# Fourth mW1 unit expanded in place inside the first pair's second layer, and three more block products of that pair's first layer at two levels

## The chip, the cores and the metric

The kernel runs on one core of one Trainium2 chip. Its engines are TensorE (PE: matmuls; PEld: the loading of its weights), VectorE (DVE), ScalarE (ACT), GpSimd (POOL) and SyncE (SP, which only issues DMAs). Each executes its own queue in order and waits on semaphores for the others. The metric is the device time of one execution in microseconds (us); lower is better. All data are fp32.

## The reference, cut to what matters

The input x is four sequences of 512 tokens by 512 values. A conditional block is followed by an adapter per sequence:

```python
q, k, v = x @ Wq, x @ Wk, x @ Wv
attn = softmax(q k^T * V**-0.5)
attn_out = (attn @ v) @ Wp + bp
cms = gelu(attn_out @ cW1 + cb1) @ cW2 + cb2      # 512 -> 2048 -> 512
cms = cms + one_hot(target_codes)
modifier = gelu(concat(attn_out, cms) @ mW1 + mb1) @ mW2 + mb2   # 1024 -> 2048 -> 512
x = clip(x + cms + modifier, 0, 1)
# adapter, its weights picked by stream[b]
h = x + gelu(x @ Wd + bd) @ Wu + bu
out = layernorm(h) * g + b
```

## The kernel before

**Products.** Nearly every large matrix product is done in the Strassen-Winograd way: the operands are cut into 2 by 2 blocks, and seven block products replace eight. Each block product needs sums of weight blocks (made by `weight_sums`, L239 to L244) and sums of token blocks (`token_sums`, L249). The seven products have the numbers 1 to 7. Three of them (1, 2, 4) take a plain weight block; 3, 5, 6 and 7 take a sum. "Two levels" means that a block product is itself cut into seven smaller ones, which takes inner sums of both operands. Sums of the weights for several layers are made once by POOL (the "expansion", `expand`, L378 to L410), in units of 256 weight columns or rows, written to DRAM (`c1_inner`, `c1_outer`, `c2_kept`, `m1_kept`, `m2_kept`) and loaded again by SP when they are used. Four weight tiles, `wslot0` to `wslot3`, are used in turn (`next_weights`).

**Order of the work.** First comes the attention of all four sequences, in two pairs. Then, for each pair of sequences, four layers: c1 (`c1_layer`, cW1), c2 (`second_layer`, cW2), m1 (`m1_layer`, mW1) and m2 (`second_layer`, mW2). The adapters of the first pair run inside the second pair's c1, those of the second pair at the end. Within c1 the products come in the order `FIRST_C = (2, 1, 5, 6, 7, 3, 4)`, in c2 and m2 in the order (3, 1, 5, 6, 7, 2, 4), in m1 in the order (1, 5, 6, 7, 2, 3, 4).

**c1.** For the first pair, products 1 and 5 have two levels (`c1_two_level`, matmuls at L1229, 28 of 256 columns); 2, 6, 7, 3 and 4 have one (matmuls at L1319, 16 of 512 columns). For the second pair (`more`) all seven have two levels. There, the inner weight sums of 1, 2 and 5 are loaded from DRAM, those of 6, 7, 3 and 4 are made by POOL when they are needed (L1221), and the inner token sums are made by POOL too (L1168 to L1171); for the first pair the token sums are made by DVE (L249). `seven` (L592, L657) combines the partial products in PSUM with DVE and ACT; `combine_first_tile` (L1334) does it for the one-level products.

**Expansion.** `expansion()` has POOL expand cW1, two units of cW2 and four units of mW1. It runs beside the attention and the first pair's c1: after each step of c1 two steps of it are put into the program (`steps(between, 2)`). `late_expansion()` expands mW2 during the first pair's m1, and after it the inner sums of cW1's product 2 for the second pair (`expand_c1_late`, `C1_KEPT`). In the profiled execution, POOL works on the fourth mW1 unit from 296.5 to 336 us, and on nothing from then to 408 us.

**Second layers.** `second_operands` forms four difference blocks of the hidden values in place (L1407) and, for each product, the inner token sums (L249 into slots 4 to 7). In the first pair's c2 (`busy`) DVE makes all of these; in the other second layers the first difference is a negated copy by ACT to which a DMA adds the other block (L1447), and in the second pair's c2 POOL makes the first inner sums. The partial products are combined by DVE (`inner`, L1091), which empties the PSUM banks: seven per product, eight in all. The temporary of `inner` is the tile `mod[0]` in c2 and `first` in m2 and m1.

**Adapters.** `load_adapter` (gathers at L1559) issues 14 indirect DMAs on POOL's queue for each sequence, into slots 4 and 5 for one and 6 and 7 for the other, at the end of the first pair's m2. Those slots are m2's token sums until then.

**Queues.** A scheduler orders the instructions of each engine, except where `keep_in_program_order` or `issue_after` pins them. DMAs are issued on SP's queue (weights, attention results), ACT's and POOL's (expansion, adapters). An engine's queue isn't left for a later instruction while the one ahead of it waits.

Of the kernel before, what the change touches and what calls it, by code (L numbers as in the profile page):

```python
# [18 lines left out]
def kernel(  # L19
# [226 lines left out]
    def token_sums(b11, b12, b21, b22, t1, t2, t3, t4, eng=None, pinned=False):  # L246
# [12 lines left out]
    C1_BESIDE = (6, 7, 3, 4)  # L259
    C1_KEPT = (2,)  # L260
# [4 lines left out]
        for p, n in ((1, 1024), (5, 2048), (2, 1024))  # L265
# [35 lines left out]

    def expand_c1_late(raws, sums):

        units = [(p, u) for p in C1_KEPT for u in range(2)]

        def block_of(i):
            return raws[i % 4].rearrange("p (m c n) -> p m c n", m=2, c=2)

        def load(i):
            p, u = units[i]  # L310
            raw = block_of(i)
            if p in C1_SUM:
                nc.gpsimd.dma_start(out=raw, in_=c1_outer[u][:, C1_SUM[p]])
            else:
                for m in range(2):
                    nc.gpsimd.dma_start(out=raw[:, m], in_=c1_plain(p, u, m))

        def begin():
            for i in range(min(4, len(units))):
                load(i)  # L320

        def rest():
            for i, (p, u) in enumerate(units):
                raw = block_of(i)
                to = sums[i % 4].rearrange("p (k n) -> p k n", k=4)
                weight_sums(
                    raw[:, 0, 0], raw[:, 0, 1], raw[:, 1, 0], raw[:, 1, 1],
                    *(to[:, k] for k in range(4)),
                )
                if i + 4 < len(units):  # L330
                    load(i + 4)
                nc.gpsimd.dma_start(out=c1_inner[p, u], in_=sums[i % 4])
                yield

        return begin, rest()

# [112 lines left out]
    def expansion():  # L451

        c2_units = [(cW2, False, c2_kept, u) for u in range(2)]
        yield from expand_c1(0, lambda: load_c1(1, nc.gpsimd))
        yield from expand_c1(1, lambda: load_raw(cW2, False, 0, slot[4:6]))

        constants()
        yield from expand_all(
            c2_units + m1_units, slot[4:6], (flat(part), slot[3], slot[1]), flat(first)
        )  # L460

    def late_expansion():

        spaces = (flat(mod[0]), flat(mod[1]), slot[0])
        quarters = lambda tiles: [t[:, at : at + 1024] for t in tiles for at in (0, 1024)]
        begin, rest = expand_c1_late(quarters(slot[6:8]), quarters(spaces[:2]))
        yield from expand_all(m2_units, slot[6:8], spaces, None, begin)
        yield from rest
# [510 lines left out]
    for pair in range(B // 2):  # L979
# [78 lines left out]

        pair_product(lhs_vp, operands, attn, bp_c, then=then, at=pT[0] if pair else None)
# [7 lines left out]

    turns = [0]

    def next_weights():  # L1070
        turns[0] += 1
        return wslot[turns[0] % len(wslot)]
# [37 lines left out]
    def inner_operands(t, half, sums, eng=None, pinned=False):  # L1110

        b11, b12 = t[:, :half, :256], t[:, :half, 256:]
        b21, b22 = t[:, half:, :256], t[:, half:, 256:]
        t1, t2, t3, t4 = sums
        token_sums(b11, b12, b21, b22, t1, t2, t3, t4, eng, pinned)
        return {1: b11, 2: b21, 3: b22, 4: t4, 5: t1, 6: t2, 7: t3}

# [28 lines left out]
    in_rows = [t.rearrange("p (c n) -> p c n", c=4) for t in slot]  # L1146

    def load_attn(pair, slots=(0, 1)):
        for k, i in enumerate(slots):
            nc.sync.dma_start(out=in_rows[i], in_=attn_kept[2 * pair + k])  # L1150

    def c1_operands(slots=(0, 1, 2, 3)):


        at0, at1, t12, t34 = (in_rows[i] for i in slots)
        b11, b12, b21, b22 = at0[:, 0:2, :], at1[:, 0:2, :], at0[:, 2:4, :], at1[:, 2:4, :]
        t1, t2, t3, t4 = t12[:, 0:2, :], t12[:, 2:4, :], t34[:, 0:2, :], t34[:, 2:4, :]
        operands = {1: b11, 2: b21, 3: b22, 4: t4, 5: t1, 6: t2, 7: t3}

        def inner_sums(p, k, eng=None):  # L1160

            s = mod[1][:, 2 * k : 2 * k + 2, :].rearrange("p a (b n) -> p (a b) n", b=2)
            t = operands[p]
            s1, s2, s3, s4 = (s[:, i : i + 1, :] for i in range(4))
            if eng is None:
                return inner_operands(t, 1, [s1, s2, s3, s4], pinned=True)
            c11, c12, c21, c22 = t[:, :1, :256], t[:, :1, 256:], t[:, 1:, :256], t[:, 1:, 256:]
            eng.tensor_tensor(s1, c12, c11, ALU.subtract)  # L1168
            eng.tensor_tensor(s2, c22, s1, ALU.subtract)
            eng.tensor_tensor(s3, c22, c12, ALU.subtract)  # L1170
            eng.tensor_tensor(s4, c21, s2, ALU.subtract)  # L1171
            return {1: c11, 2: c21, 3: c22, 4: s4, 5: s1, 6: s2, 7: s3}

        def minus(out_, one, two):
            tc.keep_in_program_order(nc.vector.tensor_tensor(out_, one, two, ALU.subtract))

        minus(t1, b12, b11)

        def rest():
            minus(t2, b22, t1)  # L1180
            yield
            minus(t3, b22, b12)
            minus(t4, b21, t2)
            yield

        return operands, inner_sums, rest()

    def fetch(out, in_):

        tc.keep_in_program_order(nc.sync.dma_start(out=out, in_=in_))  # L1190

    def c1_two_level(p, h, rhs, after, beside):


        a = []
        for g in range(2):
            w = next_weights()
            if p == 5:
                fetch(out=w, in_=c1_inner[5, g])
            else:  # L1200
                if p in C1_SUM:
                    fetch(
                        out=w[:, :1024],
                        in_=c1_outer[g][:, C1_SUM[p]].rearrange("p m c n -> p (m c n)"),
                    )
                else:
                    for m in range(2):
                        fetch(
                            out=w[:, 512 * m : 512 * m + 512].rearrange("p (c n) -> p c n", c=2),
                            in_=c1_plain(p, g, m),  # L1210
                        )
                if p not in C1_BESIDE:
                    fetch(out=w[:, 1024:], in_=c1_inner[p, g])
            a.append(w.rearrange("p (k n) -> p k n", k=8))
        if p in C1_BESIDE:
            for out_, one, two, op in (
                (4, 2, 3, ALU.add), (5, 4, 0, ALU.subtract), (6, 0, 2, ALU.subtract),
                (7, 1, 5, ALU.subtract),
            ):
                for w in a:  # L1220
                    nc.gpsimd.tensor_tensor(w[:, out_], w[:, one], w[:, two], op)  # L1221
# [55 lines left out]
    def c1_layer(h, rhs, after, more, beside):  # L1277
# [11 lines left out]
        for p in FIRST_C:  # L1289
# [8 lines left out]
            for g in range(2):  # L1298
# [31 lines left out]
                if more:  # L1330
                    beside()
# [552 lines left out]
```

## Time and profile before

| | |
|---|---|
| median of 10 runs | 1163.84 us (1162.45 to 1164.31) |
| the profiled execution's own time | 1164.57 us |
| its span, first to last instruction | 1162.8 us |
| granted clock of TensorE, mean | 0.998 |
| first pair: c1 | 236.9 to 329.8 us |
| first pair: c2 | 329.8 to 416.4 us |
| first pair: m1, then m2 | 416.4 to 585.8, to 670.3 us |
| second pair: c1, with the first pair's adapters | 670.3 to 786.0 us |
| second pair: c2 | 786.0 to 870.6 us |
| longest wait of PE | 1.8 us, in the first pair's c2 |

The page of a profile has, in this order: the busy time of each engine, the span in 40 slices, the DMA queues, the chain of work that ended last, the costliest groups of instructions and the DMA issues. A group or a row of a timeline names the line of the kernel, the engine, the operation, the tile written and the tiles read, the shape and the count. An idle time in brackets names what ended it. A matmul of the program appears as two instructions (fp32). The name of a tile without its number stands for all tiles of the name: `wslot` for the four weight tiles, `wide` for slots 0 and 1.

### The profile page before, as it was taken

Reading aid. Unit: us, or ns where it says so; the run is one execution under the profiler, and the core shown is the slowest. Engines: PE = TensorE matmul, PEld = TensorE weight load, DVE = VectorE, ACT = ScalarE, POOL = GpSimd, SP = SyncE. Lnnn points to the kernel's source line nnn. Section 1 sums busy time; section 2 is a strip of 40 time slices with the busy share of each in tenths; the row PEclk is TensorE's granted clock in tenths of the full one; section 3 lists DMA queues with packets and bytes.
Section 4 is the critical chain, followed back from the end, with each engine's and each line's share of the span. In section 5 each row is a group of like instructions: output and inputs, shape, how many; then the busy total and the mean of one; then the engine's idle time right before and its main releaser. Section 6 shows DMA issues by size and latency. Waiting matters only on the chain.

```text
span 1162.8 us, 13672 instructions
## 1 busy us (share of the span) xinstructions
PE 1153.0 (99%) x4941; PEld 922.4 (79%) x4941; DVE 884.9 (76%) x1227; ACT 293.7 (25%) x535; POOL 587.6 (51%) x646
## 2 busy tenths in 40 slices
PE   9999999999999999999999999999999999999997
PEld 8588468566468888888888877778888888888875
DVE  6755755477699965898699956789994588689955
ACT  4234426235520000013310036372000003230014
POOL 4999979898950058864200767971000001165401
PEclk9999999999999999999999999999999999999999
DMA  9795494898775578897837562145645364675701
GB/s 281 266 251 198 183 395 153 337 371 284 270 268 235 170 264 315 302 336 304 262 130 305 177 205 91 65 163 196 265 160 184 145 237 161 185 268 199 252 2 72
DMA packets 101442, 258.88 MB, mean 223 GB/s; under 512 B 24532, under 2 KB 59648, under 8 KB 86144
## 3 DMA queue, kind: packets, MB, share of 16 engines
q1 hardware_dynamic: 77088, 157.17, 38.6%
q0 software_dynamic: 20848, 89.18, 21.6%
q10 hardware_dynamic: 3440, 11.67, 2.5%
q8 instruction: 39, 0.64, 0.2%
q14 instruction: 27, 0.22, 0.1%
HBM read 188.78 MB, written 66.06 MB: 219 GB/s over the span
## 4 chain that ended last, share of the span: by engine, by line
PE 95%; DVE 3%; DMA 1%; issue 1%; DVEq 0%
PE i L1387 28%; PE i L1487 28%; PE sum L748 10%; PE sum L1229 9%; PE sum L682 8%; PE c L1319 5%; PE down_ps L1594 2%; PE up_ps L1613 2%; DMA wslot<-in_L_cond_mW 1%; PE tr_ps L519 1%; DVE slot L249 1%; DVE wide L1407 1%; PE up_ps L1608 1%; DVE hidden L592 0%; PE tr_ps L935 0%
## 5 line engine op out<-in xcount | busy, mean ns | idle before, releaser
L1387 PE MATMUL i<-slot,wslot 128*128 128x256 f32 x1184 | 261.2, 379 | 0.1
L1387 PEld LDWEIGHTS i<-slot,wslot 128*128 128x128 f32 x1184 | 224.8, 190 | 31.2 <-DMA wslot<-in_L_cond_mW 0.5
L1487 PE MATMUL i<-slot,wslot 128*128 128x256 f32 x896 | 202.8, 379 | 1.8 <-DVE cms L1091 1.8
L1487 PEld LDWEIGHTS i<-slot,wslot 128*128 128x128 f32 x896 | 170.2, 190 | 25.3 <-DVE cms L1091 2.2
L1487 PE MATMUL i<-hidden,wslot 128*128 128x256 f32 x576 | 132.2, 379 | 0.0
L1487 PEld LDWEIGHTS i<-hidden,wslot 128*128 128x128 f32 x576 | 109.4, 190 | 15.7 <-issue 1.0
L1098 ACT COPY first<-i 128x512 f32<-128x512 f32 (+1 forms) x42 | 21.6, 515 | 390.3 <-PE i L1387 234.0
L1091 DVE TENSOR_TENSOR part<-i,part 128x512 f32<-128x512 f32 (+1 forms) x156 | 90.5, 591 | 36.9 <-PE i L1387 27.3
L1120 ACT ACTIVATE hidden<-hidden,bias 128x512 f32<-128x512 f32 x128 | 83.9, 716 | 73.7 <-DVE hidden L592 63.6
L1770 POOL DMA_DIRECT2D slot<-xT_kept x4 | 2.9, 727 | 152.9 <-PE i L1387 152.9
L1229 PE MATMUL sum<-mod,wslot 128*128 128x256 f32 x288 | 66.6, 379 | 0.0
L249 DVE TENSOR_TENSOR slot<-hidden 128x1024 f32<-128x1024 f32 x46 | 61.4, 1334 | 0.0
L1229 PEld LDWEIGHTS sum<-mod,wslot 128*128 128x128 f32 x288 | 54.7, 190 | 7.4
L1773 POOL TENSOR_TENSOR cms<-cms,slot 128x512 f32<-128x512 f32 x16 | 23.9, 1518 | 68.1 <-PE i L1387 38.5
L249 DVE TENSOR_TENSOR slot<-hidden,slot 128x1024 f32<-128x1024 f32 x46 | 56.7, 1232 | 0.3
L1091 DVE TENSOR_TENSOR part<-i,first 128x512 f32<-128x512 f32 (+1 forms) x50 | 31.4, 631 | 31.8 <-PE i L1387 20.8
L1319 PE MATMUL c<-slot,wslot 128*128 128x512 f32 x128 | 55.3, 592 | 0.0
L378 POOL DMA_DIRECT2D slot<-in_L_cond_mW x24 | 17.8, 750 | 73.3 <-DVE slot L249 72.3
L592 DVE TENSOR_TENSOR sum<-sum,wslot 128x512 f32<-128x512 f32 x48 | 33.2, 695 | 26.3 <-PE sum L748 18.6
L748 PE MATMUL sum<-hidden,wslot 128*128 128x256 f32 x232 | 53.2, 379 | 0.0
L592 DVE TENSOR_TENSOR hidden<-part,hidden 128x2048 f32<-128x2048 f32 x20 | 50.2, 2510 | 0.5
L1319 PEld LDWEIGHTS c<-slot,wslot 128*128 128x128 f32 x128 | 24.3, 190 | 30.6 <-issue 27.7
(342 smaller groups left out, 2147.8 us busy)
## 6 DMA issues: line engine op xcount, KB each, us to landing
wslot<-m_kept SPq DMA_DIRECT2D x48, 1024.0 KB, 6.4
wslot<-m_kept SPq DMA_DIRECT2D x36, 512.0 KB, 4.8
wslot<-c_kept SPq DMA_DIRECT2D x16, 1024.0 KB, 6.3
slot<-in_L_cond_mW POOLq DMA_DIRECT2D x24, 512.0 KB, 7.6
wslot<-in_L_cond_mW SPq DMA_DIRECT2D x24, 512.0 KB, 6.4
wslot<-in_L_cond_cW SPq DMA_DIRECT2D x40, 256.0 KB, 4.9
slot<-in_L_cond_cW POOLq DMA_DIRECT2D x12, 512.0 KB, 6.7
m_kept<-wide POOLq DMA_DIRECT2D x6, 1024.0 KB, 9.0
```

The costliest lines, as they stand in the source:

```text
L249: i = eng.tensor_tensor(out_, one, two, ALU.subtract)
L592: nc.vector.tensor_tensor(dst, a, b, ALU.add)
L682: nc.tensor.matmul(ps, lhsT=lhs[p][:, c, r * P : (r + 1) * P], rhs=rhs[p][:, c, :], start=(first_ and c == 0), stop=(c == 1), skip_group_c ...
L748: nc.tensor.matmul(v[:, j, :], lhsT=lhs[p][:, c, j * P : (j + 1) * P], rhs=rhs[p][:, c, :], start=(first_ and j == 0 and c == 0), stop=(c ...
L1091: nc.vector.tensor_tensor(dst, ps, other, ALU.add)
L1120: nc.scalar.activation(block[:, t, :], block[:, t, :], AF.Gelu, bias=bias_c[:, 8 * half + t : 8 * half + t + 1],)
L1229: nc.tensor.matmul(halves_of(ps)[:, j, :], lhsT=a[g][:, at_[q], j * P : (j + 1) * P], rhs=rhs[q][:, 0, :], start=(first_ and j == 0), stop ...
L1319: nc.tensor.matmul(ps, lhsT=lhs(c, t), rhs=operands[p][:, c, :], start=(c == 0), stop=(c == 1),)
L1387: nc.tensor.matmul(out_ps[:, j, :], lhsT=a[j][q][:, c, :], rhs=now[q][:, c, :], start=(c == 0), stop=(c == 1),)
L1487: nc.tensor.matmul(ps[:, :256], lhsT=a[k // 2][q][:, k % 2, :], rhs=now[q][:, k, :], start=(k == 0), stop=(k == 3),)
L1594: nc.tensor.matmul(ps, lhsT=wd[:, c, n * P : (n + 1) * P], rhs=y[:, c, tokens], start=(c == 0), stop=(c == NV - 1),)
L1773: nc.gpsimd.tensor_tensor(cms[s][:, d, :], cms[s][:, d, :], in_rows[3][:, d, :], ALU.add)
```

## The change

In the first pair's c1, the block products 2, 3 and 4 have two levels instead of one, so that only 6 and 7 keep one. Their inner weight sums are not loaded but made beside the matmuls: by DVE for 2 and 3, by POOL for 4. The weights and first sums of product 2 are started ahead of the layer (`c1_begin`): for the first pair inside the last product of the attention, for the second pair just ahead of its c1. The attention results of the first pair are loaded, and the first difference made, inside that product also.

For the second pair, the inner sums of product 2 are no longer kept in DRAM; POOL makes them when they are needed, like those of 6, 7, 3 and 4, and `expand_c1_late` goes.

`expansion()` makes three units of mW1 instead of four. The fourth is done by `expand_in_place`: its raw weights are loaded into `mod[0]` and `mod[1]` at the start of the first pair's c2, and its sums are made in place and in slots 2, 3 and 0. A gate (a DVE memset of one column of slot 2 at the sixth product, `GATE`) stands ahead of five of its seven steps in the program; two are put into m1. The temporary of `inner` is `first` in the first pair's c2, since `mod[0]` holds the raw weights.

The first pair's c2 begins as the second pair's does (`busy` goes): ACT and an adding DMA form the first difference, and POOL makes the first inner sums.

The diff, cut to its core (functions that were only moved are left out):

```diff
-    C1_BESIDE = (6, 7, 3, 4)
-    C1_KEPT = (2,)
+    C1_BESIDE = (
+        {2: nc.vector, 3: nc.vector, 4: nc.gpsimd},
+        {p: nc.gpsimd for p in (2, 6, 7, 3, 4)},
+    )
+    GATE = 5
+    C1_TWO = ((2, 1, 5, 3, 4), (2, 1, 5, 6, 7, 3, 4))
...
-            c2_units + m1_units, slot[4:6], (flat(part), slot[3], slot[1]), flat(first)
+            c2_units + m1_units[:3], slot[4:6], (flat(part), slot[3], slot[1]), flat(first)
...
-        begin, rest = expand_c1_late(quarters(slot[6:8]), quarters(spaces[:2]))
-        yield from expand_all(m2_units, slot[6:8], spaces, None, begin)
-        yield from rest
+        yield from expand_all(m2_units, slot[6:8], spaces, None)
+
+    def expand_in_place():
+        u = 3
+        raw = [t for t in mod]
+        load_raw(mW1, True, u, [flat(t) for t in raw])
+        yield
+        a11, a12, a21, a22 = (
+            raw[0][:, :, :256], raw[1][:, :, :256], raw[0][:, :, 256:], raw[1][:, :, 256:]
+        )
+        lower, upper = slot[3][:, :1024], slot[3][:, 1024:]
...
+        keep(1, a11, slot[2][:, :1024], False)
+        yield
+        tt(block(lower), a21, a22, ALU.add)
+        inner_sums(block(lower), upper)
+        nc.gpsimd.dma_start(out=m1_kept[5, u], in_=slot[3])
+        yield
+        tt(a21, a11, a21, ALU.subtract)
+        tt(a11, block(lower), a11, ALU.subtract)
+        keep(6, a11, lower, True)
+        yield
+        keep(7, a21, upper, True)
+        yield
+        keep(2, a12, lower, False)
+        yield
+        tt(a12, a12, a11, ALU.subtract)
+        keep(3, a12, slot[0][:, :1024], True)
+        yield
+        keep(4, a22, slot[0][:, 1024:], False)
+        yield
...
+    def c1_weight_sums(a, eng):
+        for out_, one, two, op in (
+            (4, 2, 3, ALU.add), (5, 4, 0, ALU.subtract), (6, 0, 2, ALU.subtract),
+            (7, 1, 5, ALU.subtract),
+        ):
+            for w in a:
+                i = eng.tensor_tensor(w[:, out_], w[:, one], w[:, two], op)
+                if eng is nc.vector:
+                    tc.keep_in_program_order(i)
+
+    def c1_begin(rhs, more):
+        _, inner_sums, _ = rhs
+        a = c1_weights(2, nc.vector)
+        c1_weight_sums(a, C1_BESIDE[more][2])
+        return a, inner_sums(2, 0, nc.gpsimd if more else None)
...
+            def operands_c1():
+                load_attn(0, (6, 7))
+                c1_rhs.extend(c1_operands((6, 7, 0, 2)))
+            then = {
+                6: [operands_c1], 4: [lambda: c1_begun.extend(c1_begin(c1_rhs, False))]
+            }
...
+                    if (p, g, t) == (7, 1, 1):
+                        weights[3] = c1_weights(3, nc.vector)
+                        c1_weight_sums(weights[3], nc.vector)
...
-        made = second_operands(h, pair == 0, nc.gpsimd if final else None)
+        made = second_operands(h, nc.gpsimd)
         between = expanding if pair == 0 else extra
-        for _ in c1_layer(h, c1_rhs, made[2], final, lambda: steps(extra, 1)):
+        if final:
+            c1_begun = c1_begin(c1_rhs, True)
+        for _ in c1_layer(h, c1_rhs, c1_begun, made[2], final, lambda: steps(extra, 1)):
...
-        def beside_c2(i, pair=pair):
+        last_unit = iter(()) if final else expand_in_place()
+
+        def beside_c2(i, pair=pair, last_unit=last_unit):
+            if i == 0:
+                next(last_unit, None)
+            elif i == GATE and pair == 0:
+                tc.keep_in_program_order(nc.vector.memset(slot[2][:, :1], 0.0))
+                for _ in range(5):
+                    next(last_unit)
...
-        for _ in second_layer(made, cW2, c2_kept, blocks_of(cms), c_last(pair), None, beside_c2):
+        for _ in second_layer(
+            made, cW2, c2_kept, blocks_of(cms), c_last(pair), None, beside_c2,
+            mod[0] if final else first,
+        ):
...
         for i, _ in enumerate(m1_layer(h, m1_made, m1_rhs[0], made[2])):
-            if i > 1:
+            if i == 1:
+                for _ in last_unit:
+                    pass
+            elif i > 1:
                 steps(between, 3)
```

## The prediction, on record before the changed kernel was run

> **What bounds the kernel now.** I read the busy row of the page first, then what TensorE (PE) waited for, then the engines in order of time. Times are microseconds (us).
>
> ```profile
> PE 1153.0 (99%) x4941; PEld 922.4 (79%) x4941; DVE 884.9 (76%) x1227; ACT 293.7 (25%) x535; POOL 587.6 (51%) x646
> ```
>
> PE is busy for 1153.0 of 1162.8. The time is the sum of the matmuls, and only two things change it: fewer matmul columns, or a wait that stops PE. The view of what PE waited for has one line inside the work:
>
> ```profile
> PE i L1487 <- DVE cms L1091: 1.8, 1, 1.8
> ```
>
> The stretch of PE that the change rewrites, in order of time (start, length, what):
>
> ```profile
> 236.91 13.90 PE L1319 MATMUL c<-slot,wslot 128*128 128x512 f32 x32
> 250.64 1.89 PE L1229 MATMUL sum<-slot,wslot 128*128 128x256 f32 x8
> ...
> 262.73 1.89 PE L1229 MATMUL sum<-wide,wslot 128*128 128x256 f32 x8
> ...
> 274.81 13.90 PE L1319 MATMUL c<-wide,wslot 128*128 128x512 f32 x32
> ```
>
> A one-level block product lasts 250.64 - 236.91 = 13.73, a two-level one 262.73 - 250.64 = 12.09. The starts meet: no gap. What matters as much is POOL's queue where the second pair begins, with PE beside it:
>
> ```profile
> 648.68 1.07 POOL L1559 DMA_INDIRECT slot<-in_L_cond_W_down,idx_d  x1 [3.40 <-DVE mod L1091]
> ...
> 668.89 0.95 POOL L1559 DMA_INDIRECT slot<-in_L_cond_W_down,idx_d  x1 [0.30 <-PE i L1487]
> ...
> 686.74 0.95 POOL L1559 DMA_INDIRECT slot<-in_L_cond_ln_b,idx_e  x1 [0.30 <-issue]
> 687.71 0.74 POOL L1168 TENSOR_TENSOR mod<-slot 128x256 f32<-128x256 f32 x1
> ```
>
> ```profile
> 670.25 1.89 PE L1229 MATMUL sum<-wide,wslot 128*128 128x256 f32 x8
> 671.97 3.62 PE L1229 MATMUL sum<-mod,wslot 128*128 128x256 f32 x16
> ```
>
> POOL issues the gathers of two adapters, 14 each, from 648.68 to 687.71 without a break: 20.2 for the first 14, 18.8 for the second. The second pair's first product starts at 670.25 in their midst. Before, it needs nothing from POOL there: its weight sums come from memory, its token sums were made at 633 to 645.
>
> **The change, part by part.**
>
> *(a) Matmuls.* In the first pair, products 2, 3 and 4 go from 13.73 to 12.09: 3 x 1.64 = **-4.9**, all on PE. Nothing else on PE changes in number.
>
> *(b) The old wait.* PE's 1.8 at 345 comes from VectorE (DVE) starting the first pair's second layer late: it makes that layer's first token sums itself. The change gives these to POOL and forms the first difference with a negated copy on ACT and an adding DMA, as the second pair has it already, and there PE runs without a gap from 786 to 871. I take **-1.8**; bounds -1.8 and 0.
>
> *(c) Start of the first layer.* Product 2 now needs, for its second step, eight weight sums and a token sum on DVE. In DVE's new order they stand behind the attention product's last combination (before: 233.67 + 0.6 = 234.3). PE needs them at 236.91 + 1.73 = 238.6. POOL's expansion runs beside them, and both read SBUF twice:
>
> ```profile
> 235.41 0.95 DVE L249 TENSOR_TENSOR mod<-slot 128x256 f32<-128x256 f32 x1
> ...
> 248.20 0.41 DVE L249 TENSOR_TENSOR mod<-wide,mod 128x256 f32<-128x256 f32 x1
> ...
> 316.82 5.64 DVE L1407 TENSOR_TENSOR wide<-hidden,hidden 128x2048 f32<-128x2048 f32 x1
> 322.38 0.68 DVE L592 TENSOR_TENSOR hidden<-c,hidden 128x512 f32<-128x512 f32 x1
> 322.98 2.28 DVE L1407 TENSOR_TENSOR hidden<-hidden,hidden 128x2048 f32<-128x2048 f32 x1
> ```
>
> A sum of 256 alternates with POOL at 0.88 from start to start, and takes 0.33 alone. Nine at 0.88, less 0.9 for a DMA issue of POOL's in between and the first at 0.33: 234.3 + 6.9 = 241.2, **+2.6**. At 0.33 each it is 0 (237.3); with one long wait as at 316.82 (5.64 - 2.28 = 3.4) it is 6. I take alternation, the nearest row.
>
> Products 3 and 4 cost no wait: 3's weight sums run on DVE near 297, when POOL's last unit of expansion is over (296.5 before, where the removed fourth unit begins), and POOL's sums for 4 have about 3 to spare. DVE has 18 operations of 0.6 and four of 0.34 in a product of 12.09; the second pair's product 4 (774 to 786) carries the 18 and PE does not wait. The cover is thin, about 1.
>
> *(d) Expansion in place, early part.* The gate holds back less than it names: it is a write to the first column of slot 2, and in the changed program POOL's order runs five sums of 256 and two of 1024 that don't touch that column as soon as the raw block lands (about 11 after the second layer starts, from 7.6 for such a load). That is 5 x 0.69 + 2 x 2.3 = 8.0 of POOL beside a full DVE:
>
> ```profile
> 354.00:366.00 12.00, 12.00 (x57) 10.55 (x57) 11.83 (x15) 0.37 (x1) 0.00 (x0) 1.00 0.67 264
> ```
>
> (The stretch, its length, then busy time of PE, weight loads, DVE, ACT and POOL.) DVE needs 361.13 - 349.43 = 11.7 of each 12.09, so it can't catch up. PE may run 3.45 into the next product before it needs a bank that DVE empties; by the second pair's rows 1.3 of that is spare. About 5.4 of the 8.0 meets sums that read SBUF twice (the rest falls beside reads of PSUM): 5.4 - 1.3 = **+4.1**. Lower bound 0 (the load lands late, POOL's ops fall into DVE's PSUM time); upper 8, all of it in front of DVE.
>
> The Trainium skill (SBUF — State Buffer, Who interferes with whom) says the pair shared by DVE and GpSimd is locked for one instruction and that issue order decides who blocks. It speaks against this part of the change. But by it a DVE sum waits for one POOL sum, 0.7, and the row at 316.82 waited 3.4, through five: by the rule (d) is about 4, by that row near 8.
>
> *(e) Later part.* After the gate POOL does seven sums of 256 and one of 1024, 7.1; DVE is about 4 ahead of need there (second pair: emptied by 859.3, needed at 862). **+1**, bounds 0 and 3. The m1 layer's extra sums are nearly paid by the two late cW1 units that go (8 x 0.7). The unit's data are in time: its first sums land near 407, and are needed 12 after the layer ends.
>
> *(f) The second pair's first product.* Its weight sums are no longer kept, so POOL makes eight, and in the changed program's POOL order they are split: the first adapter's 14 gathers, three sums for the first weight tile, **the second adapter's 14 gathers, and only then** the second tile's sums. PE's second step on that tile waits for them and PE executes in order. 668.89 + 3 x 0.7 + 18.8 + 0.7 = 690.5; PE is there at 671.97 + 0.86 = 672.8. **+17.6**. The gathers wait for m2's operand slots, so they move with PE, and an earlier shift doesn't help. Bounds: all at the quickest pitch seen, 1.26, give 648.68 + 28 x 1.26 + 2.8 - 672.8 = 14; with DVE delaying the sums, 20.
>
> *(g) The clock.* After the last matmul the granted clock falls to half (0.52 from 1159.0; PE ended near 1156). At the kernel's start 16 matmuls of 128 columns take 3.57 and the next 16 take 2.31, against 1.75 later: 1.8 + 0.6 = **+2.4** after a wait as long as (f). Bounds 0 and 2.5.
>
> The skill (TensorE: Matmul & The Clock Gate, What's actually happening) has the clock at half after an idle window of about 3.4 us until such a window was busy. By that (g) would be an estimated 1.7.
>
> **Sum.** -4.9 - 1.8 + 2.6 + 4.1 + 1 + 17.6 + 2.4 = **+21.0**. Against the profiled execution's own 1164.57 (span 1162.8 and 1.8 around it) that is 1185.6; the median of the runs is 0.7 lower, so I predict **1184.8**. All low ends: -6.7 + 14 = +7.3, 1171; all high ends: -4.9 + 6 + 8 + 3 + 20 + 2.5 = +34.6, 1198.
>
> **Rivals.**
> *1. No wait at the second pair, the change pays (not slower).* The mechanism is POOL's queue at the second pair's start: if the second tile's sums were done by 672.8, only (a) to (e) count. That needs 28 gathers in 672.8 - 648.7 - 2.8 = 21.3, 0.76 each. For it: POOL is only issuing, and the sums are short. Against: no gather took under 1.25 from start to start. With (c) and (d) at 0 to 4 the time is 1157 to 1163; the change breaks even where the wait at (f) is about 6.7 less what (c) to (e) take. Chance 0.06.
> *2. The same, but contention takes the gain.* No gather wait, (c) to (e) at 7.7 or more: 1163 to 1172. For it: DVE at 11.83 of 12. Chance 0.05.
> *3. DVE starved throughout.* (f) as forecast, and long waits as at 316.82 in (c), (d) and in m1, where DVE is at 23.7 of 24 from 487 to 535: 1193 to 1205. Against: many of DVE's operations there read PSUM, and PE didn't wait in m1 before. Chance 0.10.
> The forecast, with (f) and moderate contention, 1172 to 1193: 0.79.
>
> **How the numbers follow.** Range 1172 to 1195: it leaves out rival 1, most of 2 and the upper end of 3. What a measurement of this kernel can tell from no change is about 0.2%, 2.3 us. Faster by more than that: 0.05, from rival 1. Within: 0.03, from rivals 1 and 2. Slower: 0.92.
>
> **What would show it.** Right: one PE wait of 14 to 20 at the second pair's first product, released by POOL, behind 14 gathers, and a lower granted clock just after it; products 2, 3, 4 of the first pair at 12.1; no wait at the second layer's second product from late sums, but waits of some us there from DVE beside POOL's 1024-wide sums; two to three us at the first layer's second step. Wrong: PE dense through 670 to 700, which means (f) was misread in POOL's queue; or no lengthened DVE sums in the second layer, which means that the contention was overpriced.

## The result, and the profile after

The change makes the kernel slower: 1199.45 us (median of 9 runs, 1193.93 to 1210.92) against 1163.47 (31 runs), a ratio of 1.0325 with an interval of 1.0302 to 1.0347. The prediction was 1184.8 with a range of 1172 to 1195: the right sign, and too small. The profiled execution took 1195.38, with a span of 1193.6: 30.8 more than the span before, where the prediction had 21.0. It is one of the short runs; what the median has beyond it, 4.1, can't be put to a place.

The experiments ran on several chips. On two of them the kernel before takes 1178 to 1180 itself, so each experiment below is compared with runs of the kernel before on its own chip, and by the lengths of its stages.

The page's busy row after, and what PE waited for (total, times, longest):

```profile
PE 1157.2 (97%) x5013; PEld 939.6 (79%) x5013; DVE 927.8 (78%) x1279; ACT 295.9 (25%) x539; POOL 614.2 (51%) x655
```

```profile
PE sum L1259 <- POOL wslot L566: 15.9, 1, 15.9
PE sum L1259 <- DVE mod L249: 3.6, 1, 3.6
PE i L1406 <- DVE part L1203: 2.6, 1, 2.6
PE sum L1259 <- DVE sum L699: 2.2, 4, 0.7
PE i L1406 <- DMA wslot<-in_L_cond_mW: 1.5, 2, 1.3
```

Before, this view had one line inside the work, 1.8. Now one wait stands out, and it is the one that was forecast. But the three behind it add up to 8.4, waits for weight loads to 1.5 (smaller ones are left out here), and the busy time of PE rose by 4.2 although its matmuls became shorter: that is matmuls at half clock. A stage's length, from the start of its first matmul to that of the next stage's, tells where the 30.8 went:

| | before | after | difference |
|---|---|---|---|
| first pair, c1 | 92.8 | 100.0 | +7.2 |
| c2 | 86.7 | 86.0 | -0.7 |
| m1 | 169.2 | 175.9 | +6.7 |
| m2 | 84.6 | 84.6 | 0 |
| second pair, c1 | 115.8 | 133.9 | +18.1 |
| the rest | | | -0.5 |

**Second pair's c1.** POOL's queue, and PE beside it, in the changed kernel (start, length, what, and in brackets the idle time and what ended it):

```profile
681.56 2.09 POOL L566 TENSOR_TENSOR wslot<-wslot 128x256 f32<-128x256 f32 x3
683.81 0.97 POOL L1573 DMA_INDIRECT slot<-in_L_cond_W_down,idx_d  x1 [0.16 <-issue]
...
700.25 0.95 POOL L1573 DMA_INDIRECT slot<-in_L_cond_ln_b,idx_e  x1 [0.31 <-issue]
701.22 3.44 POOL L566 TENSOR_TENSOR wslot<-wslot 128x256 f32<-128x256 f32 x5
```

```profile
685.12 1.03 PE L1259 MATMUL sum<-mod,wslot 128*128 128x256 f32 x4
702.01 4.50 PE L1259 MATMUL sum<-mod,wslot 128*128 128x256 f32 x12 [15.86 <-POOL wslot L566]
```

Three sums, 14 gathers from 683.81 to 701.22, then the sums that PE waits for: as forecast, with 15.9 for 17.6. The 12 matmuls behind it take 4.50 instead of some 2.7, at half clock.

**First pair's c1.** The start of the layer, PE and then DVE:

```profile
236.88 1.89 PE L1259 MATMUL sum<-slot,wslot 128*128 128x256 f32 x8
242.32 6.49 PE L1259 MATMUL sum<-mod,wslot 128*128 128x256 f32 x16 [3.55 <-DVE mod L249]
```

```profile
234.26 7.58 DVE L566 TENSOR_TENSOR wslot<-wslot 128x256 f32<-128x256 f32 x8
241.77 0.41 DVE L249 TENSOR_TENSOR mod<-slot 128x256 f32<-128x256 f32 x1
```

Eight sums take 7.58 together, but they are far from equal: one 1.33, three 0.94 or 0.95, three 0.41, and the last

```profile
239.12 2.73 DVE L566 TENSOR_TENSOR wslot<-wslot 128x256 f32<-128x256 f32 x1
```

beside three sums of POOL without a gap (239.47 to 241.54). The 16 matmuls behind the wait take 6.49; 16 of this form took 3.62 before (row 671.97 of the prediction). The stretches of that time show why (length, busy time of PE, PEld, DVE, ACT and POOL, then the granted clock, and the share and rate of the DMAs):

```profile
241.00:242.00 1.00, 0.00 (x0) 0.00 (x0) 1.00 (x2) 0.00 (x0) 0.55 (x1) 0.58 0.96 393
244.00:246.00 2.00, 2.00 (x6) 1.55 (x6) 2.00 (x1) 0.00 (x0) 2.00 (x4) 0.50 0.97 397
248.00:250.00 2.00, 2.00 (x11) 1.77 (x10) 1.90 (x3) 0.29 (x1) 2.00 (x2) 1.00 0.95 381
```

The clock falls inside the wait and stays at 0.50 for 6.8 in all, until 248: 5.7 of it with PE at work, which is about 2.8 lost on top of the wait.

**m1.** The longest wait, 2.6, stands behind one DVE sum that took 5.08; POOL beside it:

```profile
521.85 5.08 DVE L249 TENSOR_TENSOR slot<-cms 128x512 f32<-128x512 f32 x1
```

```profile
521.30 2.37 POOL L358 TENSOR_TENSOR slot<-slot,mod 128x1024 f32<-128x1024 f32 x1
...
526.33 0.79 POOL L375 DMA_DIRECT2D m_kept<-slot  x1
```

Five sums of POOL without a gap (four of 256 from 523.62 on), and the DVE sum is done at 526.93, when POOL has come to a DMA issue. This is the row 316.82 of the prediction again, in a place where PE had only little work left in front of it. The clock fell just behind the wait (527.88) and stayed at half for 3.4, which is 1.7 lost. With the 1.5 for weight loads, late in the layer, that is 5.8 of the 6.7.

### The profile page after: what moved, and what is told of

Its sections match the earlier page's. It is cut to its first block, busy times and chain, and to the rows that moved or that the text cites. A ratio compares the mean times of both kernels' runs of the same rounds, so it can differ in the third digit from the quotient of the medians.

```text
span 1193.6 us, 13934 instructions
## 1 busy us (share of the span) xinstructions
PE 1157.2 (97%) x5013; PEld 939.6 (79%) x5013; DVE 927.8 (78%) x1279; ACT 295.9 (25%) x539; POOL 614.2 (51%) x655
## 4 chain that ended last, share of the span: by engine, by line
PE 86%; DVE 9%; DMA 2%; issue 2%; POOL 1%; ACT 0%; DVEq 0%; POOLq 0%
PE i L1406 26%; PE i L1501 25%; PE sum L855 10%; PE sum L1259 9%; PE sum L789 8%; PE down_ps L1608 2%; DVE slot L249 2%; PE up_ps L1627 2%; PE c L1349 2%; DVE hidden L1426 1%; DVE hidden L699 1%; DMA wslot<-in_L_cond_mW 1%; DVE wslot L566 1%; PE tr_ps L626 1%; DVE sum L699 1%
## 5 line engine op out<-in xcount | busy, mean ns | idle before, releaser
L1210 ACT COPY first<-i 128x512 f32<-128x512 f32 (+1 forms) x49 | 24.2, 494 | 456.5 <-PE i L1406 242.8
L1203 DVE TENSOR_TENSOR part<-i,part 128x512 f32<-128x512 f32 (+1 forms) x156 | 90.7, 591 | 38.7 <-PE i L1406 29.7
L1259 PE MATMUL sum<-mod,wslot 128*128 128x256 f32 x384 | 94.5, 395 | 23.0 <-POOL wslot L566 15.9
L1259 PEld LDWEIGHTS sum<-mod,wslot 128*128 128x128 f32 x384 | 75.5, 198 | 36.6 <-POOL wslot L566 16.3
L249 DVE TENSOR_TENSOR slot<-hidden 128x1024 f32<-128x1024 f32 x44 | 56.7, 1288 | 0.0
L699 DVE TENSOR_TENSOR sum<-sum,mod 128x512 f32<-128x512 f32 x72 | 48.2, 690 | 10.4 <-PE sum L1259 9.7
L1203 DVE TENSOR_TENSOR part<-i,first 128x512 f32<-128x512 f32 (+1 forms) x56 | 33.9, 608 | 27.4 <-PE i L1406 16.8
L699 DVE TENSOR_TENSOR hidden<-sum,hidden 128x512 f32<-128x512 f32 x66 | 42.9, 679 | 13.9 <-ACT hidden L1277 7.7
L699 DVE TENSOR_TENSOR hidden<-part,hidden 128x2048 f32<-128x2048 f32 x20 | 53.2, 2661 | 0.5
L566 POOL TENSOR_TENSOR wslot<-wslot 128x256 f32<-128x256 f32 x48 | 36.6, 787 | 26.4 <-DMA wslot<-in_L_cond_cW 23.7
```

Source lines behind the costliest of these rows:

```text
L249: i = eng.tensor_tensor(out_, one, two, ALU.subtract)
L566: i = eng.tensor_tensor(w[:, out_], w[:, one], w[:, two], op)
L699: nc.vector.tensor_tensor(dst, a, b, ALU.add)
L1203: nc.vector.tensor_tensor(dst, ps, other, ALU.add)
L1210: nc.scalar.copy(c1, p1)
L1259: nc.tensor.matmul(halves_of(ps)[:, j, :], lhsT=a[g][:, at_[q], j * P : (j + 1) * P], rhs=rhs[q][:, 0, :], start=(first_ and j == 0), stop ...
```

## The experiments

The runs are called by the first letters of their names. The theory I set out with: four separate losses (POOL's queue at the second pair; DVE's weight sums at the start of c1 and the half clock after the wait; DVE's sums for product 3; POOL's shifted expansion in m1). The rivals: one cause for all, the unit in place; or waits that only move. "Chip A" is the kind on which the kernel before takes 1163, "chip B" the kind on which it takes 1178 to 1180. All stage lengths are worked out as in the table above, each from one profiled execution. The times are medians; b_before_again is a single run.

| run | chip | time, and ratio to before | first c1 | c2 | m1 | second c1 |
|---|---|---|---|---|---|---|
| before | A | 1163.5 | 92.8 | 86.7 | 169.2 | 115.8 |
| changed | A | 1199.5, 1.0325 | 100.0 | 86.0 | 175.9 | 133.9 |
| b_before_again | B | 1177.3 | 92.8 | 84.6 | 169.2 | 130.5 |
| a_after_again | B | 1207.0, 1.0266 | 100.3 | 86.0 | 170.8 | 135.1 |
| e1_sums_kept | B | 1194.7, 1.0141 | 106.5 | 85.4 | 170.0 | 125.8 |
| e2_unit_early | B | 1207.2, 1.0245 | 109.2 | 84.6 | 174.2 | 134.8 |
| e3_sums3_pool | B | 1197.0, 1.0132 | 103.5 | 86.0 | 169.2 | 135.0 |
| e4_two_one_level | B | 1192.2, 1.0092 | 102.0 | 85.4 | 170.9 | 136.1 |
| c_kept_one2_pool3 | B | 1183.3, 1.0036 | 97.9 | 86.0 | 172.1 | 128.7 |
| d_pool_first_sums | B | 1184.8, 1.0051 | 92.8 | 91.2 | 170.7 | 130.9 |
| f_gathers_later | A | 1187.0, 1.0193 | 102.9 | 86.0 | 177.1 | 119.9 |
| h_no_dve_weight_sums | A | 1188.6, 1.0229 | 95.8 | 86.0 | 169.3 | 134.5 |
| k_best | A | 1161.6, 1.0000 | 90.4 | 85.4 | 169.6 | 115.6 |
| l_best_two_levels | B | 1204.0, 1.0224 | 120.1 | 85.4 | 169.8 | 125.4 |

**The queue at the second pair: e1 and f.** In e1 the sums of product 2 are kept in DRAM again, by `expand_c1_late` as it was before the change:

```diff
-        {p: nc.gpsimd for p in (2, 6, 7, 3, 4)},
+        {p: nc.gpsimd for p in (6, 7, 3, 4)},
+    C1_KEPT = (2,)
```

> The changed kernel, but the second pair's product-2 weight sums are made early and kept in DRAM again, as before the change. Theory (four separate losses, the largest of them POOL's queue behind the gathers): PE's 16 us wait at the second pair's second step goes, and with it the half clock that follows (1.7), so about 17.7 us less than the changed kernel: 1177 to 1183; the first pair keeps its own waits (3.6 at the first layer, about 3 in m1). Rival (the wait only moves on, since the token sums of the next product stand behind the same gathers): 5 to 10 us less, 1187 to 1194, with a new wait at the second pair's next product.

The second pair's c1 came down to 125.8, against 135.1 of the changed kernel on such a chip, and PE had other waits there (3.7 and 2.2). That fits neither theory as a whole: the 9.3 less is of the rival's size, but the new waits stand in the same product and not in the next. So the kernel before was profiled again, on such a chip:

> The kernel before, unchanged, for a second profile, because its time on the chip of the first four experiments was 1180.0 and not 1163.5. If it takes 1163 to 1165 here, its one wait of 1.8 and the stage times 92.8, 86.6, 169.2, 84.6 and 115.8 stay. If it takes about 1180 here, the extra 16 must stand as waits of PE, and then they bound what the changed kernel's waits owe to the chip: waits at the start of the second pair's first layer (115.8 before) if loads are late behind the gathers, or half clock.

There it waits too, without any sum of POOL's in the way (PE, then DVE):

```profile
676.85 1.13 PE L1229 MATMUL sum<-wide,wslot 128*128 128x256 f32 x4 [2.36 <-issue]
688.30 3.60 PE L1229 MATMUL sum<-mod,wslot 128*128 128x256 f32 x8 [10.32 <-DVE sum L592]
```

```profile
681.25 0.69 DVE L592 TENSOR_TENSOR mod<-sum,mod 128x512 f32<-128x512 f32 x1 [9.69 <-remote]
```

DVE is idle for 9.69, and for 4.93 more ahead of its next sum, and the view names no releaser of this core ("remote"), although the matmuls whose results it reads had begun by 677. ACT and POOL have such idle times there too. All of it lies beside the second adapter's gathers or just behind them. So on chip B this stretch costs the kernel before about 14.7 as well (130.5 - 115.8), and the changed kernel is only 4.6 longer there. What causes it was not tried. The question was put again on chip A, by order alone: the weight sums are begun ahead of the second adapter's gathers.

```diff
-            load(0, 6)
             c1_rhs = next_rhs[0]
+            c1_begun = c1_begin(c1_rhs, True)
+            load(0, 6)
```

> The changed kernel, but the second pair's product-2 weights are begun ahead of the second adapter's gathers in the program, so that in POOL's queue only four of these 14 gathers are left in front of the second tile's sums. Theory (POOL's queue alone makes the 16 to 17.5 us wait): the wait shrinks to 1 to 5, that is four gathers at 1.26 less what PE has behind it, no half clock follows or only a short one, and the second pair's first layer takes 116 to 122 instead of 133.9 to 135.1. Rival (the start of this layer is held by something else too, as in the unchanged kernel on these chips, which waits 13 there with no sum of POOL's in the way): the layer still takes 126 to 131.

```profile
PE sum L1259 <- POOL wslot L566: 2.7, 1, 2.7
```

133.9 became 119.9, and the wait 2.7 instead of 15.9, with two gathers instead of 14 between PE's first two steps on POOL's queue. The theory holds: on chip A the wait comes from POOL's queue, and another order of it takes 13.2 of the 15.9 away.

**Is it the unit in place? e2.**

```diff
-            c2_units + m1_units[:3], slot[4:6], ...
+            c2_units + m1_units, slot[4:6], ...
-        last_unit = iter(()) if final else expand_in_place()
+        last_unit = iter(())
```

> The changed kernel, but the fourth mW1 unit goes back into the expansion beside the attention and the first layer (no expansion in place, no gate). Theory (separate losses): m1 loses its 2.6 to 3 us wait and the half clock after it and is back near 169 us, against 175.9; the second layer gets back about 1; the first layer is dearer by 1 to 4, because POOL now works beside DVE's weight sums for product 3; the 16 us wait at the second pair stays. Net 2 to 6 us less than the changed kernel, 1190 to 1197. Rival (contention set loose by the unit in place is the main loss, and makes the spread between runs): 10 us less or more, with runs within 4 us of each other.

The second layer got back 1.4 (84.6), as the theory had it. But m1 kept a wait of 3.0 without the unit (174.2), so that wait is not the unit's; here the theory fell. And c1 rose to 109.2, with waits of 4.7 and 3.9 in products 3 and 4, where POOL now works beside DVE. The rival fell too: nothing was gained. In this profile, taking the unit out of c1 is the part of the change that gives DVE air there.

**Weight sums for product 3: e3. Product 2: e4.**

```diff
-        {2: nc.vector, 3: nc.vector, 4: nc.gpsimd},
+        {2: nc.vector, 3: nc.gpsimd, 4: nc.gpsimd},
```

> The changed kernel, but POOL instead of DVE makes the weight sums of product 3 in the first pair's first layer; POOL is idle from 288 to 302 there. Theory (DVE has no room for eight more sums in a 12.09 us product): the waits in products 3 and 4 of that layer (about 1.0 + 1.8 + 1.1 + 1.0) shrink and the first layer gets 2 to 4 us shorter than its 100.2; 1191 to 1197 in all. Rival (DVE and POOL share the port, so it is one whoever makes the sums): within 1 us of 100.2.

```diff
-    C1_TWO = ((2, 1, 5, 3, 4), (2, 1, 5, 6, 7, 3, 4))
+    C1_TWO = ((1, 5, 3, 4), (2, 1, 5, 6, 7, 3, 4))
```

> The changed kernel, but product 2 of the first pair's first layer has one level again (13.73 of matmuls instead of 12.09, no weight sums and no inner token sums for it). Theory (the 3.6 us wait sets off 6.8 us at half clock): the wait and the half clock go, the matmuls cost 1.64 more, so the layer is about 5 us shorter than its 100.2, 95 in all, and the granted clock stays at 1.00 from 237 to 250. Rival (the half clock has another cause, or the wait moves to product 1, whose inner token sums DVE now makes at the same place): the layer is shorter by 2 or less.

In e3 the three waits of products 3 and 4 (1.4, 0.7 and 0.6 in the changed kernel) shrank to one of 0.6, and the two products took 25.0 instead of 28.3, so that term was right; but the layer as a whole was not shorter (103.5), because waits of 1.2, 2.6, 1.0 and 0.8 stood in products 1 and 5, where the first profile had 0.3 and 0.6. In e4 the wait at the layer's start went, but a wait of 5.3 came at product 5, and the layer was not shorter (102.0). That is the rival, with the wait in product 5 and not in 1. Both say that the waits move.

**Do they move by themselves? a.** The changed kernel once more:

> The changed kernel, unchanged, for a second profile and for the spread between its runs (1194 to 1211). Theory (several thin covers, each of which holds or not by the phase of POOL against DVE, and half clock after each long wait): the 16 us wait at the second pair is there again within 1.5 us, while the waits of the first pair's first layer and of m1 differ in place and size from the first profile by several us. Rival (one cause that is fixed in the program): the same waits at the same places within 0.5 us, and the spread comes from somewhere else.

The wait at the second pair is 17.2. In c1 most waits are where they were (3.8 at the start, and the three of products 3 and 4); one in product 1 grew from 0.3 to 0.9. There the rival is right, but e1 is not with it: in its first c1 DVE executes the same instructions in the same order as in the changed kernel, and the layer took 106.5. A sum of 256 that took 1.07 in the first profile (at 253.34) took 3.75 there (at 252.73). But m1 takes 170.8, and its wait stands near the layer's start (1.3), not at 102 of its 176 us. Over the ten profiles with the unit in place, m1 took 169.2 to 177.1. In all of them, and in the kernel before, the longest DVE sum of m1 takes 4.3 to 6.6 us, where the widest ones alone take 2.3. In b_before_again one of 6.16 did not make PE wait: it counts only where PE has little work left in front of it.

**The parts that should pay: c, d, k, l.** In c, product 2 has one level, its sums for the second pair are kept, and POOL makes the sums of product 3 (the edits of e1, e3 and e4 together):

> The changed kernel with three of its parts taken back: the second pair's product-2 weight sums are kept in DRAM, product 2 of the first pair's first layer has one level, and POOL makes the weight sums of product 3. What stays of the change: products 3 and 4 of the first pair at two levels, the unit expanded in place, the first difference by ACT and a DMA. Theory (separate losses): 17.7 less for the second pair, about 5 for product 2, about 2 for product 3, so some 24 less than the changed kernel on the same chip, and within 6 us of the kernel before. Rival (the unit in place starves DVE whatever the rest does): still 10 or more above the kernel before, with waits in the second layer and in m1.

1.0036 times before (1.0013 to 1.0060). The median is 23.6 less than the changed kernel's on this chip, near the 24 forecast, but that is luck: in the profiles the second c1 is 6.4 less and not 17.7, the first 2.4 and not 7. PE waits 5.2 in product 5. DVE and POOL in this run:

```profile
267.13 5.38 DVE L249 TENSOR_TENSOR mod<-wide,mod 128x256 f32<-128x256 f32 x1
```

```profile
266.86 0.57 POOL L400 DMA_DIRECT2D m_kept<-wide  x1
267.45 0.74 POOL L242 TENSOR_TENSOR slot<-slot,slot 128x256 f32<-128x256 f32 x1
...
269.50 2.33 POOL L397 TENSOR_TENSOR first<-slot,slot 128x1024 f32<-128x1024 f32 x1
271.77 0.55 POOL L400 DMA_DIRECT2D m_kept<-slot  x1
```

This DVE sum, and the one ahead of it (264.57, 2.64), come through when POOL issues a DMA (271.77 and 266.86), and the combinations that PE waits for stand behind them, from 272.43 on. The change puts the next product's token sums into the middle of the running product's combinations (`prepare` at step 3). In k they are moved to where no combination stands behind them:

```diff
-                    then = {3: [lambda: prepare(i + 1)]}
+                    then = {}
+                    if p == 1:
+                        prepare(i + 1)
+                    elif p == 3:
+                        then = {3: [lambda: prepare(i + 1)]}
...
                 c1_two_level(p, h, ready[p], weights[p], after, then)
+                if p == 5 and not more:
+                    prepare(i + 1)
```

> The parts of the change that should pay, alone: products 3 and 4 of the first pair's first layer at two levels with both products' weight sums on POOL, the unit expanded in place, the first difference by ACT and a DMA; product 2 at one level, the second pair's sums kept in DRAM, and the inner token sums made where no combination of the running product stands behind them (for product 5 ahead of product 1, for product 3 behind product 5). Theory: the 5.6 us wait and the half clock behind a DVE sum that waited 5.4 for POOL (in the run of c_kept_one2_pool3) go: the first layer takes 89 to 91 against 92.8 of the kernel before, and the whole is 1 to 4 less than the kernel before on the same chip. Rival (a DVE sum of two SBUF operands finds another run of POOL to wait for wherever it stands): the first layer takes 94 or more, and the whole is slower than the kernel before.

What PE waited for in k, but for 1.1 at the kernel's very start:

```profile
PE sum L1305 <- DVE sum L745: 0.6, 1, 0.6
PE i L1568 <- DVE cms L1249: 0.5, 1, 0.5
```

c1 is 90.4: 92.8 less two products at 1.64, one wait of 0.6, and 0.3. (c was profiled on chip B and k on chip A; the c1 of the kernel before and of the changed one differ by 0.3 or less between them.) The sums still wait for POOL there (one takes 2.71 at 246.88), but product 2 at one level leaves DVE nothing to combine until 254, and PE does not wait. The whole is 1161.6 against 1162.7, a ratio of 1.0000 (0.9986 to 1.0015): the best version found, not to be told from the kernel before; the 1 to 4 less of the theory did not come. Then l, which is k with product 2 at two levels again, its weight sums on DVE and product 1's token sums in the middle of its combinations, as in the change:

> The kernel of the run k_best (first layer 90.4, no wait at its start) with one thing added: product 2 of the first pair's first layer at two levels, its eight weight sums on DVE, as in the change. Theory (these sums, each waiting for POOL's expansion, cost more than the 1.64 of matmuls they save): PE waits 3.5 to 5 at the second step and then runs 3.4 to 7 us at half clock, so the layer takes 94 to 98 and the whole is 3 to 8 more than k_best. Rival (the wait was the fault of the other changes around it): the layer takes 89 to 90, and the whole is 1 to 2 less than k_best.

c1 takes 120.1: 29.7 more than in k, almost four times the upper end of what was expected (98 - 90.4); the theory has the sign and not the size. DVE, then POOL:

```profile
234.48 7.88 DVE L608 TENSOR_TENSOR wslot<-wslot 128x256 f32<-128x256 f32 x8
...
246.44 8.64 DVE L561 TENSOR_TENSOR wide<-slot,wide 128x1024 f32<-128x1024 f32 x1
```

```profile
246.96 2.36 POOL L397 TENSOR_TENSOR part<-slot,slot 128x1024 f32<-128x1024 f32 x1
...
251.56 2.33 POOL L397 TENSOR_TENSOR slot<-part,slot 128x1024 f32<-128x1024 f32 x1
253.85 1.80 POOL L239 TENSOR_TENSOR part<-slot 128x256 f32<-128x256 f32 x1
```

One sum that lasts 1.2 elsewhere (244.07 in k) takes 8.64: three POOL sums of 1024 go first. Only then does the chain of combinations go on (at 255.00), and PE waits 7.7 there and 10.4 some 18 us later, where token sums and differences of DVE have met POOL's next runs (5.35 at 261.87, 3.37 at 274.90, 3.49 at 278.19). The weight sums themselves keep DVE for 7.9, hardly more than in the changed kernel (7.6). I read the rest as what that delay makes DVE meet; no run separates the two.

**The weight sums left out: h.** The changed kernel without DVE's sums for products 2 and 3; its output is not that of the block any more:

> The changed kernel, but DVE's 16 weight sums for products 2 and 3 of the first pair's first layer are left out (these products then use stale sums; all else is computed). Theory (the DVE sums are what makes PE wait there: 3.6 to 4.2 at the second step and the half clock after it, and 3 to 4 in products 3 and 4): the first layer takes 88 to 92 instead of 100.0 to 103.5. Rival (the token sums and DVE's lag behind POOL cost as much without the weight sums): 95 or more.

95.8: the rival's side. The wait and the half clock at the start are gone, but waits of 1.9, 2.0, 1.2 and 0.8 stand in products 1 and 5, more than the 0.3 and 0.6 of the first profile. So the sums are a part of the loss in c1, and DVE's lag with the token sums is another.

**The second layer's start: d.** The kernel before, with that part of the change alone:

```diff
-        made = second_operands(h, pair == 0, nc.gpsimd if final else None)
+        made = second_operands(h, False, nc.gpsimd)
```

> The kernel before, with one thing of the change: the first pair's second layer begins as the second pair's does (first difference by ACT and an adding DMA, first inner sums by POOL). Theory: PE's 1.8 wait there goes and nothing takes its place, 1.5 to 2 less than the kernel before. Rival (POOL, still at the fourth mW1 unit until 336 there, makes the sums late): 1 to 8 more than the kernel before, with a wait at the second layer's start.

c2 rose to 91.2: POOL is at the fourth unit until 330 and makes the sums late (PE waits 4.4 for them). The rival holds: the step needs POOL to be through with the unit when c2 starts. In the changed kernel the unit has left that queue. In e2 it hasn't, but c1 is 9 us longer there than in the changed kernel and POOL is through at 322.5, 24 before c2 starts; c2 then takes 84.6. Whether the step gains anything is not shown: c2 takes 85.4 to 86.0 with it and with the unit in place, 86.7 and 84.6 in the two profiles of the kernel before.

## Why the prediction was off, step by step

| term | predicted | in the first profile |
|---|---|---|
| (a) matmuls | -4.9 | -4.9 (k, with two of the three products: 90.4 less its wait of 0.6 is 89.8, where 92.8 - 3.3 = 89.5) |
| (b) old wait | -1.8 | -2.1 (86.7 - 84.6), but see below |
| (c) first c1 | +2.6 | +12.1 (100.0 less 92.8 - 4.9) |
| (d) second layer | +4.1 | +1.4 (86.0 - 84.6) |
| (e) m1 | +1 | +6.7 |
| (f) POOL's queue | +17.6 | +15.9 |
| (g) clock after it | +2.4 | +1.7 |

**Right.** The mechanism, place and size of (f): 18.1 of the 30.8 with (g), read from the order of POOL's queue and the pitch of the gathers; f showed that this order is the cause. (g) is 1.7: the half clock lasts until 705.4 and PE works from 702.0, which is half of 3.4. (a) holds.

**(b) has its size by luck.** The 1.8 were put down to DVE making the first token sums itself. b_before_again is the same program, on a chip of the other kind: DVE makes the same sums, and PE has no such wait (c2 84.6). What differs is the difference sum of the prediction's row 316.82, which took 5.64:

```profile
316.87 2.28 DVE L1407 TENSOR_TENSOR wide<-hidden,hidden 128x2048 f32<-128x2048 f32 x1
```

What follows it on DVE comes 3.3 earlier. So the old wait was one meeting with a run of POOL, which comes in one execution and not in another, and the change can't be credited with taking it away.

**(c) failed, in three places.** The first is the price "I take alternation, the nearest row": three of the eight sums did alternate (0.94), three ran alone (0.41), and the last was held for 2.73 through three sums of POOL. That the wait is 3.6, not far from 2.6, is luck. (The terms of that sum, 8 x 0.88 + 0.33 - 0.9, also give 6.5 and not 6.9.) The second is the clock: I counted a loss only after the long wait of (f), and not after this one; it lost 2.8 more. The third is "Products 3 and 4 cost no wait": the sums for 3 ran on DVE from 305 to 312, not near 297, and took 6.92, and the two products took 28.3, 4.1 more than 2 x 12.09; e3 took 3.3 of that away. The remaining 1.6 of the 12.1 stands in products 2, 1 and 5, 0.9 of it as two waits.

**(e) failed, though not by its own mechanism.** It priced the unit. What m1 lost is a wait of 2.6 behind one held DVE sum, 1.7 of half clock behind it, and 1.5 for weight loads, whose cause was not followed. e2 has a wait of 3.0 in m1 without the unit, and ten profiles with it have an m1 of 169.2 to 177.1. What I missed is that a shift of POOL's expansion against DVE moves the places where DVE is held, and that m1, with DVE at 23.7 of 24 from 487 to 535, has little cover against it.

**(d) was overpriced, by its cover.** c2 is 0.8 to 1.4 longer with the unit than without it (e2). POOL ran its five sums of 256 and two of 1024 about where they were expected, and both engines were held (POOL, then DVE):

```profile
346.68 4.70 POOL L243 TENSOR_TENSOR slot<-mod 128x256 f32<-128x256 f32 x1 [6.76 <-DMA mod<-in_L_cond_mW]
```

```profile
359.71 4.43 DVE L1426 TENSOR_TENSOR hidden<-hidden,wide 128x2048 f32<-128x2048 f32 x1
```

The POOL sum, 0.7 alone, ran beside DVE's two differences of 2048 (346.31 to 350.79). The DVE difference, 2.3 alone, and the sums around it (from 352.90 to 378.8) took about 5.2 longer than alone, near the 5.4 of the prediction. But PE waited only 1.1 for it (at 379.58). The step that failed is "1.3 of that is spare": the lead of DVE covered about 4.

**The rivals.** What came is rival 3 (1193 to 1205, chance 0.10): the long wait as forecast, and DVE held for long in c1, in c2 and in m1. My argument against it, that "PE didn't wait in m1 before", was no evidence: sums of 4.3 stand in m1 before, too, and only their places were harmless. The range should have reached to its end.

**The spread.** The changed kernel's runs lie within 17 us, those of the kernel before within 4.5. The run of 1193.9 has a mean granted clock of 0.990, that of 1210.9 one of 0.983. That is 2 x 0.010 x 1192.1 = 24 us and 2 x 0.017 x 1209.1 = 41 us at half clock. PE loses at most half of the difference, about 9, to the clock; the rest of the 17 must be more waits. This fits waits that come and go with the phase of POOL against DVE, each with a piece of half clock; but no run of the long kind was profiled, so it is argued and not shown.

## What to carry to other kernels

Before work is added to an engine's queue, read that queue across the stage's border: 14 gathers between two halves of one step's sums cost 16 us here, and another order of the same work took 13 of them away. Where two engines contend, a sum is not priced by its length and not by alternation: it can cost as much as the longest run of the other engine that it meets, and what that costs depends on what stands behind it in its own queue. Put such sums where nothing that PE needs stands behind them (c to k: 97.9 to 90.4). An engine that fills 98% of a stretch hardly catches up, so it is the lead it has that covers a delay: in c2 about 5.2 of delay cost PE 1.1, in m1 one sum held for 4.4 cost 2.6. And one profile in which it caused no wait shows only that its delays fell in harmless places: take a second profile before a small wait is explained.

## What the runs showed of the hardware that I had not expected

A DVE sum of two SBUF operands was held through a whole run of POOL sums: 5.08 through five, 5.38 through four (one of them of 2.33), 8.64 through three of 2.34. It works the other way too: a POOL sum of 0.7 took 4.70 behind DVE. In the same stretches others alternate with POOL at 0.94. The Trainium skill (SBUF — State Buffer, Who interferes with whom) says that the shared pair is locked for one instruction and that issue order decides. That one engine is held over several instructions of the other in a row agrees with neither the price by this rule (0.7 or 2.3) nor a fair alternation; the measured rows decide. When it is one and when the other, these runs don't show.

The granted clock fell to half during a wait of 3.6 (c1) and already during one of 2.7 (the second c1 of f) and 0.2 behind one of 2.6 (m1), while another wait of 2.6 in f (265.0 to 267.6) did not lower it. The stretches at half clock last 3.4, 6.8, 10.2, 13.7 or 17.1 in these runs. The Trainium skill (TensorE: Matmul & The Clock Gate, What's actually happening) has a free-running window of about 3.4 and half clock after an idle one. The lengths, multiples of 3.4, agree; two of the waits that sufficed (2.6 and 2.7) are shorter than the window.

The unchanged kernel takes about 15 us longer on some chips, and in the two profiles from them in which the second pair's c1 is unchanged (b_before_again and d) the time is lost in the first 20 us of that layer, where DVE and ACT stand still at once, PE behind them, and the view names no releaser. This stays open.
